# A four-layer graph network on one core: four pieces of work moved in the issue order

## The chip, the cores and the metric

The kernel runs on one core of a Trainium2 chip. The metric is the device time of one execution in microseconds (us), lower is better. All times below are from executions on the chip.

## The reference

The program takes `x` of 128 batches x 64 nodes x 256 features and an adjacency matrix `adj` (64 x 64), all float32. Four layers follow each other, each of the form

```python
h = jnp.maximum(_layernorm(x, axis=-1), 0.0)
x = x + layer(h)
```

Layer 0 is a graph convolution with batch normalization. Layer 1 multiplies with the eigenvectors of a normalized Laplacian, which the kernel computes itself. The change touches layers 2 and 3. Layer 2 is

```python
h = relu(einsum('ts,bsh->bth', adj, x @ Wg0 + bg0))
h = relu(einsum('ts,bsh->bth', adj, h @ Wg1 + bg1))
for p in range(1, 5):
    nw = 64 // p                      # windows of p consecutive nodes
    last = lstm(Wih[p-1], Whh[p-1], bias, h[:, :nw*p].reshape(-1, p, 256))   # the last state
    h = h.at[:, arange(nw)*p + (p-1)].set(last)
```

where the LSTM has gates i, f, g, o and zero initial state. So for p=1 each window is one node and needs the gates i, g and o alone, and for p=4 there are four cells in sequence. Layer 3 is an attention over 512 edges (`src`, `dst`) with 4 heads:

```python
Xq, Xv = H @ W_lin.T, H @ W_val.T                    # per head
e = (leaky_relu(Xq[src] + Xq[dst]) * a).sum(-1) + log(adj[src, dst] + 1e-8)
attn = exp(e - segment_max(e)[src]) / segment_sum(exp(..))[src]
Y = segment_sum(attn * Xv[dst], src)                 # then Y @ W_out.T
```

## The kernel before, in words

The 128 x 64 rows of `x` are kept in SBUF as 16 blocks of 512 rows (`NB` = 16 blocks, 8 batches each, tiles `X`), and are handled by block. In layer 2 they are also kept feature-major: `nodes(q)` gives a quarter of the batch (32 batches) as 128 features x 2 x 64 nodes x 32. A float32 product of two 256-wide operands is made from seven partial products instead of eight; they are made in the order 1, 6, 7, 5, 2, 4, 3 into four PSUM banks, with additions on VectorE (DVE) between. The sums of the operand that the seven products need are made ahead on DVE.

Instructions are recorded by a framework that orders them per engine by data dependencies and by the order in which they are written down. The wrapper `Ordered`/`Engines` stands around the engines, so that nearly all instructions of TensorE (PE), DVE and ScalarE (ACT) have one line in the profile, L800. `nc.mark()` returns the last instruction recorded on each of these three engines, and `nc.hold(marks)` makes what is recorded from then on go behind the marked one on its engine, without a semaphore.

The stages that matter:

- **Layer 2's two mixes** (`layer2`, to about 671 us). `block(i)` forms `g` of block i by the seven products with `W0` (`seven`; the last three products and their additions lie in the function `rest` that it returns, into the banks `ps` and `pe`), mixes block i-1's second half over the graph (`features(i-1)`, 16 small matmuls from `y` into `ps`), and multiplies `g` by `W1` into the bank `pt`, which gives `y`.
- **The LSTM** (`windows`, 671 to 1733 us). Its PSUM pools are `lsps` with seven banks, tile `ps`, and `lstps` with one bank, tile `pt`. For p=1, `single` handles the chunks in eight pairs; each pair has three groups of gates, and the multiplications of the cells lie on GpSimd (POOL). For p=2, 3 and 4, `lstm(p, t, ch, Ws)` is one cell of one chunk. It starts with the first sums `T` (tile `ls_tx`: one 128x512 and two 128x256 subtractions) of the nodes at step t, then makes the gates i and g, then o and f. The chunks are handled in pairs, t by t. For p=4 there are two pairs, so the second has eight cells (t = 0 to 3, two chunks).
- **The ways back.** `back(i)` takes block i of layer 2's result back to rows: ACT or DVE copies it to `ls_t`, TensorE transposes it in two times four 128x128 steps into `pt`, and DVE adds each four to `X`. Blocks 0 to 7 are done behind the cells of the second pair of p=4, from the list `ways`: one behind each cell with t < 2, two behind each with t = 2, which ends the list. Blocks 8 to 15 are done in layer 3's first steps.
- **Layer 3** (`layer3`, 1733 us to the end). Its PSUM pools are `l3ps` with seven banks and `l3cps` with one bank, tile `acc`. They take the place of `lsps` and `lstps`, bank by bank. `turned(0)` transposes the normalized block `h` twice into `acc` and copies it to `hT`, and `queries(0)` makes its first products with `w_qv` in `acc`, from which `XV` and `Q` are copied; all this is recorded with high priority. Then come 32 half-block steps g: `score` (edge scores from `ed_S` and `Q`), `reduce`, the values and the output. Each eight steps close a group q: `softmax(q)` is recorded in the last step of the group, and it works on 128x512 tiles `sm_e` and `sm_m`, with scans for the segment maximum and sum, then four reciprocals of 128x128 and one multiplication. Its result is read by `edgewise(q)`, recorded two steps later.

Of the kernel before, what the change touches and what calls it, by code (L numbers as in the profile page):

```python
# [843 lines left out]
class Plan:  # L844
# [56 lines left out]
    def rest(self):  # L901

        while any(self.queue.values()):
            for e in self.queue:
                self.fill(e, 1e9)
# [8 lines left out]
class Fast:  # L914
# [89 lines left out]
    def tridiagonal(self, S, made, plan):  # L1004
# [17 lines left out]

        d = go("T", lambda: keep("p", S, self.JR[:]), [made], 0.3, 0.5)
        d = go("V", lambda: o.copy(m[:], now["p"][:]), [d], 0.15, 0.28)
        d = go("T", lambda: keep("p", self.JR[:], m[:]), [d], 0.3, 0.5)
        rest = go("V", lambda: o.copy(A[:], now["p"][:]), [d], 0.15, 0.28)
# [419 lines left out]
NB = 16  # L1446
# [20 lines left out]
class Kernel:  # L1467
# [679 lines left out]
    def layer2(self, pool, psum, ps2, ps0):  # L2147

        nc, o = self.nc, self.o
# [89 lines left out]
        def block(i):  # L2239
            if i == 2:  # L2240
                with ExitStack() as ce:
                    epool = ce.enter_context(self.tc.tile_pool(name="l3e", bufs=1, side="right"))
                    nc.hold(nc.mark())
                    self.edges(self.w3, epool, ps0)
                    nc.hold()
            if i == SEVEN - 1:
                sums0()
            a = as_.pop(i)
            g = pool.tile([P, 2, BT], F32, name="g")
            rest = (seven if i >= SEVEN else eight)(i, a, g)  # L2250
            if i:
                features(i - 1)
            rest()
            mixed(i + 1)
            y = ys[i] = pool.tile([P, TPB, D], F32, name="y")
            for jj in range(0, TPB, 2):
                p = ps2.tile([P, 2, D], F32, name="pt")
                for j in range(2):
                    for kc in range(2):
                        self.mm(p[:, j, :], g[:, kc, (jj + j) * P:(jj + j + 1) * P], W1[:, kc, :],  # L2260
                                kc == 0, kc == 1)
                o.add(y[:, jj:jj + 2, :], p[:], b1[:, None, :].to_broadcast([P, 2, D]))
            normed(i + 2)
# [3 lines left out]
    def windows(self):  # L2267

        nc, o, io = self.nc, self.o, self.io
        cx, (w, wq, gp, tp, zp, psum, pst) = self.stage([("lsw", 1), ("lswq", 1), ("lsg", 2), ("lst", 2), ("lsz", 2),
                                                         ("lsps", 7), ("lstps", 1)], "tile")
        with cx:
            bias = w.tile([P, 4, 8], F32, name="ls_b")
            bh = w.tile([P, 4, 8], F32, name="ls_bh")
            with nc.allow_non_contiguous_dma("a few values"):
                nc.sync.dma_start(bias[:], io["L2_gnn_bih"].rearrange("q (k p) -> p q k", p=P))
                nc.sync.dma_start(bh[:], io["L2_gnn_bhh"].rearrange("q (k p) -> p q k", p=P))  # L2280
            o.add(bias[:], bias[:], bh[:])
            flat = [x.rearrange("p t d -> p (t d)") for x in self.X]
            self.late = []
            self.g_ = Ring([self.X2[i][:].rearrange("p x t d -> p x (t d)") for i in (4, 5, 6, 0)])
            self.t_ = Ring([flat[i] for i in (14, 2, 3)])
            self.c_, self.h_, self.th_ = Ring(flat[12:15]), Ring(flat[8:10]), Ring(flat[10:12])
            self.u_ = Ring([flat[15][:, 0:512], flat[15][:, 512:1024]])
            self.lp = gp, tp, zp, psum, bias

            def load(ap, n, x):  # L2290

                if x is None:
                    return ([wq.tile([P, 4 * D], F32, name=f"ls_w{n}{kc}")[:] for kc in range(2)]
                            + [wq.tile([P, 2 * D], F32, name=f"ls_s{n}{i}")[:] for i in range(3)])
                return [flat[x], flat[x + 1], flat[x + 2][:, 0:512], flat[x + 2][:, 512:1024], flat[x + 3][:, 0:512],
                        flat[x + 3][:, 512:1024]]

            def weights(p):

                out = []  # L2300
                for n, m in enumerate(("Wih", "Whh") if p > 1 else ("Wih",)):
                    t = load(None, n, None if p % 2 == 0 else 4 - 4 * n)
                    ap = io[f"L2_gnn_{m}_t"][p - 1]
                    for kc in range(2):
                        nc.sync.dma_start(t[kc], ap[kc * P:(kc + 1) * P, :])
                    A = [[t[kc].rearrange("p (x k m) -> p x k m", k=2, m=P)[:, :, k, :] for kc in range(2)]
                         for k in range(2)]
                    S1, S2, S4 = (y.rearrange("p (x m) -> p x m", m=P) for y in t[2:5])
                    o.add(S1, A[1][0], A[1][1])
                    o.sub(S2, S1, A[0][0])  # L2310
                    o.sub(S4, A[0][1], S2)
                    S3 = t[5].rearrange("p (x m) -> p x m", m=P) if len(t) > 5 else A[1][0]
                    o.sub(S3, A[0][0], A[1][0])
                    out.append({1: A[0][0], 2: A[0][1], 3: S4, 4: A[1][1], 5: S1, 6: S2, 7: S3})
                return out

            ready, ways = weights(1), []
            for p in range(1, 5):
                Ws = ready
                nw = N // p  # L2320
                parts = -(-nw // 16)
                chunks = []
                for q in range(NG):
                    w0 = 0
                    for k in range(parts):
                        w1 = w0 + (nw - w0) // (parts - k)
                        chunks.append((q, w0, w1))
                        w0 = w1
                for n in range(0, len(chunks), 2):
                    if n == 2 and p < 4:  # L2330
                        ready = weights(p + 1)
                    if n == 2 and p == 4:
                        self.fetch(0, 8)
                        ways = [0, 1, 2, 3, 4, 5, 6, 7]
                    two = [dict(q=q, w0=w0, w1=w1) for q, w0, w1 in chunks[n:n + 2]]
                    two[-1]["last"] = p == 4 and n + 2 >= len(chunks)
                    if p == 1:
                        self.single(two, Ws[0], n + 2 >= len(chunks))
                        continue
                    for t in range(p):  # L2340
                        for ch in two:
                            self.lstm(p, t, ch, Ws)
                            for i in ways[:1 if t < 2 else 2]:
                                self.back(i, pst, "pt")
                            ways = ways[1 if t < 2 else 2:]
            self.fetch(8, NB)

    def fetch(self, i0, i1):
# [15 lines left out]
    def lstm(self, p, t, ch, Ws):  # L2364


        o = self.o
# [6 lines left out]
        half = lambda kc: node(kc).rearrange("p w (h b) -> p h w b", h=2)  # L2374

        T = tp.tile([P, 4, 256], F32, name="ls_tx")[:, :, 0:W].rearrange("p n (w b) -> p n w b", b=16)
        o.sub(T[:, 0:2], H[:, :, at, 16:32], half(0))
        o.sub(T[:, 2], H[:, 1, at, 16:32], T[:, 0])
        o.sub(T[:, 3], H[:, 1, at, 0:16], T[:, 2])
        parts = [(Ws[0], {1: H[:, 0, at, 0:16], 2: H[:, 1, at, 0:16], 3: H[:, 1, at, 16:32],  # L2380
                          5: T[:, 0], 7: T[:, 1], 6: T[:, 2], 4: T[:, 3]})]
        if t:
# [222 lines left out]
    def layer3(self):  # L2605
        nc, o, io = self.nc, self.o, self.io
        cx, (w,) = self.stage([("l3x", 1)], "tile")
        with cx:
# [3 lines left out]
            with cy:  # L2612
# [10 lines left out]
                st, LAG = {}, 10  # L2623
# [4 lines left out]
                for g in range(8 * NG):  # L2628
# [22 lines left out]
                    if ahead:  # L2651
                        rest = self.queries(st, ahead, WQV, *pools)
                    elif g + 2 < 8 * NG:
                        self.turned(st, g // 2 + 1, *pools)
                    if g + 6 == 8 * NG:

                        p = pools[4].tile([P, BT], F32, name="ps")
# [2 lines left out]
                        self.act_copy(self.cont[:N, :], p[:N, :])  # L2660
                    if v >= 1 and g + 1 < 8 * NG:
                        self.output(st, v - 1, WO, *pools)
                    if g % 8 == 1 and 1 < g:
                        self.edgewise(st, g // 8 - 1, *pools)
                    if ahead:
# [198 lines left out]
    def softmax(self, st, q, pool, vp, sp, rp, psum, psc):  # L2864

        nc, o = self.nc, self.o
        e, m, m2 = self.shifted(st, q, pool, vp, sp, rp, psum, psc)
        scan = nc.vector.tensor_tensor_scan
        scan(m[:], self.cont[:], e[:], 0.0, op0=ALU.mult, op1=ALU.add)
        o.stt(m[:], self.contr[:], 0.0, m[:], ALU.is_equal, ALU.mult)  # L2870
        scan(m2[:, ::-1], self.contr[:, ::-1], m[:, ::-1], 0.0, op0=ALU.mult, op1=ALU.add)
        for c in range(4):
            o.recip(m2[:, c * P:(c + 1) * P], m2[:, c * P:(c + 1) * P])
        o.mul(e[:], e[:], m2[:])
        st["e", q] = e

    def summed(self, st, q, pool, vp, sp, rp, psum, psc):

# [148 lines left out]
```

## Time and profile before

| | |
|---|---|
| three runs | 2242.88, 2247.65, 2248.61 us |
| median | 2247.65 us |
| profiled execution | 2245.05 us |
| its span, first to last instruction | 2243.3 us |
| granted TensorE clock, mean | 0.997 |

| stage | us | TensorE busy |
|---|---|---|
| end of layer 2's mixes | 655 to 671 | 15.32 of 16.00 |
| p=1 | 671 to 822 | 147.43 of 151.00 |
| p=2 | 822 to 1092 | 270.00 of 270.00 |
| p=3 | 1092 to 1566 | 473.29 of 474.00 |
| p=4 | 1566 to 1733 | 165.84 of 167.00 |
| layer 3 | 1733 to 2243.3 | 504.68 of 510.30 |

The profile is one execution, recorded by the hardware. Times in it are microseconds from the span's start. In a timeline a line has the start, the duration, the engine, the source line, the operation, output<-input with the tiles' names, the shape, and the number of like instructions in a row that it stands for; in brackets stands the idle time of the engine before it and the engine and tile that ended that. In a list of waits a line has the engine and the tile that waited, what it waited for, the total, how often, and the longest. Matmuls are pipelined, so the durations of neighbours overlap.

### The profile page before, as it was taken

The numbers are of one execution on the slowest core, as the hardware profiler recorded it, in microseconds if no ns is written. First come the engines' busy times: TensorE is split into PE (matmuls) and PEld (weight loads), VectorE is DVE, ScalarE is ACT, GpSimd is POOL, SyncE is SP. The second block draws the span as 40 slices with busy tenths as digits, with TensorE's granted clock in tenths as the row PEclk, the third lists the DMA queues.
The fourth block names the chain that finished last, engine by engine and source line by source line (L and its number), as shares of the span: only waits on it lengthen the run. The fifth ranks groups of instructions, "written<-read, shape, count | busy, mean of one in ns | idle before, by whom it ended". The sixth has DMA issues, their size and how long they took to land.

```text
span 2243.3 us, 34321 instructions
## 1 busy us (share of the span) xinstructions
PE 2201.1 (98%) x12779; PEld 1644.5 (73%) x12779; DVE 1621.7 (72%) x4128; ACT 1154.4 (51%) x2522; POOL 127.5 (6%) x186
## 2 busy tenths in 40 slices
PE   7999998999999999999999999999999999999999
PEld 4554444667997888888999999888888645555654
DVE  8877576888757776676766776666767787877767
ACT  5667865665545663444444444334436654444431
POOL 1000000000225640000000000000000000000000
PEclk9999999999999999999999999999999999999999
DMA  6000220122000010000100002000001000000001
GB/s 182 1 1 15 72 57 23 64 76 41 1 29 1 1 38 1 1 1 1 39 1 1 1 1 75 2 1 1 13 1 62 20 1 15 20 15 20 15 25 48
DMA packets 61074, 54.92 MB, mean 24 GB/s; under 512 B 15203, under 2 KB 58724, under 8 KB 60900
## 3 DMA queue, kind: packets, MB, share of 16 engines
q1 hardware_dynamic: 60900, 52.66, 7.6%
q8 instruction: 102, 1.67, 0.3%
q14 instruction: 72, 0.59, 0.1%
HBM read 35.86 MB, written 16.78 MB: 23 GB/s over the span
## 4 chain that ended last, share of the span: by engine, by line
PE 77%; DVE 5%; ACT 1%; issue 1%; POOL 0%; DVEq 0%; ACTq 0%
PE ps L800 69%; PE pt L800 4%; PE acc L800 3%; PE pe L800 1%; DVE sm_m L800 1%; DVE X L800 1%; DVE aw L800 1%; DVE XV L800 0%; POOL big L2552 0%; ACT h L800 0%; ACT X L800 0%; ACT ls_g L800 0%; DVE ls_tx L800 0%; DVE lin_s L800 0%; ACT big L800 0%
## 5 line engine op out<-in xcount | busy, mean ns | idle before, releaser
L800 PE MATMUL ps<-X,X 128*128 128x160 f32 (+2 forms) x1302 | 296.7, 329 | 1.1 <-DVE X L800 0.9
L800 ACT ACTIVATE ls_g<-ls_g,ls_b 128x512 f32<-128x512 f32 (+5 forms) x408 | 207.8, 559 | 128.3 <-DVE ls_g L800 126.2
L800 PE MATMUL ps<-z,w 128*128 128x512 f32 x512 | 255.5, 621 | 0.0
L800 ACT ACTIVATE ls_g<-ps,ls_b 128x256 f32<-128x256 f32 (+2 forms) x204 | 80.5, 437 | 303.7 <-PE ps L800 302.5
L800 PEld LDWEIGHTS ps<-X,X 128*128 128x128 f32 x1302 | 225.2, 190 | 13.0 <-DVE X L800 2.7
L800 PE MATMUL ps<-X,ls_w 128*128 128x256 f32 x640 | 190.3, 379 | 0.0
L800 PE MATMUL ps<-big,X 128*128 128x256 f32 (+2 forms) x816 | 181.4, 333 | 2.6 <-ACT ls_z L800 2.5
L800 DVE TENSOR_TENSOR ls_g<-ls_z,ps 128x512 f32<-128x512 f32 (+3 forms) x226 | 125.2, 560 | 74.2 <-PE ps L800 72.4
L800 DVE TENSOR_TENSOR aw<-at,ed_OST 128x1024 f32<-128x1024 f32 x128 | 150.1, 1217 | 28.7 <-PE ps L800 28.5
L800 ACT ACTIVATE r<-ps 128x512 f32<-128x512 f32 x256 | 129.3, 625 | 74.4 <-PE ps L800 74.3
L800 PEld LDWEIGHTS ps<-big,X 128*128 128x128 f32 x816 | 139.7, 190 | 11.6 <-ACT ls_z L800 3.5
L800 PE MATMUL ps<-ls_tx,X 128*128 128x160 f32 (+1 forms) x704 | 146.2, 307 | 0.6 <-ACT ls_g L800 0.6
L800 DVE TENSOR_TENSOR X<-ls_z,ps 128x512 f32<-128x512 f32 (+4 forms) x185 | 112.4, 608 | 42.6 <-PE ps L800 37.5
L800 PE MATMUL ps<-X,ls_s 128*128 128x256 f32 x480 | 142.7, 379 | 0.0
L800 PEld LDWEIGHTS ps<-z,w 128*128 128x128 f32 x512 | 86.9, 190 | 66.6 <-issue 59.0
L800 PE MATMUL ps<-ls_tx,ls_s 128*128 128x256 f32 x464 | 134.9, 379 | 0.9 <-DVE ls_tx L800 0.9
L800 PE MATMUL ps<-ls_tx,ls_w 128*128 128x256 f32 x464 | 133.2, 380 | 0.0
L800 PEld LDWEIGHTS ps<-X,ls_w 128*128 128x128 f32 x640 | 121.2, 190 | 16.3
L800 PE MATMUL ps<-big,ls_w 128*128 128x256 f32 x464 | 131.4, 379 | 0.0
L800 DVE TENSOR_TENSOR X<-ls_g 128x1024 f32<-128x1024 f32 (+2 forms) x92 | 97.7, 1062 | 38.1 <-ACT ls_g L800 37.9
L800 PE MATMUL ps<-ed_S,Q 64*128 64x512 f32 x512 | 121.0, 604 | 0.9 <-DVE X L800 0.9
L800 PE MATMUL ps<-aw,ed_ODT 128*32 128x512 f32 x1024 | 121.7, 593 | 0.1
(583 smaller groups left out, 4203.0 us busy)
## 6 DMA issues: line engine op xcount, KB each, us to landing
X<-in_x_dram SPq DMA_DIRECT2D x32, 512.0 KB
xs<-X SPq DMA_DIRECT2D x16, 512.0 KB
X<-xs SPq DMA_DIRECT2D x16, 512.0 KB
out_dram<-X SPq DMA_DIRECT2D x31, 256.0 KB
X<-in_L_gnn_Wih_t_dram SPq DMA_DIRECT2D x4, 512.0 KB
ls_w<-in_L_gnn_Wih_t_dram SPq DMA_DIRECT2D x4, 512.0 KB
ls_w<-in_L_gnn_Whh_t_dram SPq DMA_DIRECT2D x4, 512.0 KB
w<-in_L_gnn_W_t_dram SPq DMA_DIRECT2D x2, 512.0 KB
```

Of the source, the lines that this page charges most:

```text
L800: i = method(*a, **kw)
```

## The change

Four places are changed; the instructions stay the same in number and kind.

1. In the last block of layer 2's mixes, `rest()` is recorded ahead of `features(i - 1)` instead of behind it.
2. The first sums of the first pair of p=2 are held on DVE until what was recorded ahead of p=1's last pair is issued.
3. The four reciprocals and the multiplication of `softmax` become a function `divided`, recorded in the next step of layer 3 and held on DVE behind what was recorded there before.
4. One `back(i)` is recorded behind each of the eight cells of the last pair of p=4.

```diff
             rest = (seven if i >= SEVEN else eight)(i, a, g)
+            if i == NB - 1:
+                rest()
             if i:
                 features(i - 1)
-            rest()
+            if i < NB - 1:
+                rest()
             mixed(i + 1)
...
                     if p == 1:
+                        if n + 2 >= len(chunks):
+                            after = nc.mark()[1]
                         self.single(two, Ws[0], n + 2 >= len(chunks))
                         continue
+                    if p == 2 and n == 0:
+                        for ch in two:
+                            ch["after"] = after
                     for t in range(p):
                         for ch in two:
                             self.lstm(p, t, ch, Ws)
-                            for i in ways[:1 if t < 2 else 2]:
+                            for i in ways[:1]:
                                 self.back(i, pst, "pt")
-                            ways = ways[1 if t < 2 else 2:]
+                            ways = ways[1:]
...
         T = tp.tile([P, 4, 256], F32, name="ls_tx")[:, :, 0:W].rearrange("p n (w b) -> p n w b", b=16)
+        self.nc.hold((None, ch.get("after"), None))
         o.sub(T[:, 0:2], H[:, :, at, 16:32], half(0))
         o.sub(T[:, 2], H[:, 1, at, 16:32], T[:, 0])
         o.sub(T[:, 3], H[:, 1, at, 0:16], T[:, 2])
+        self.nc.hold()
...
+                    if g % 8 == 0 and g:
+                        self.divided(st, g // 8 - 1)
                     if g % 8 == 1 and 1 < g:
                         self.edgewise(st, g // 8 - 1, *pools)
...
         scan(m2[:, ::-1], self.contr[:, ::-1], m[:, ::-1], 0.0, op0=ALU.mult, op1=ALU.add)
+        st["e", q], st["sums", -1] = e, m2
+
+    def divided(self, st, q):
+
+        nc, o, e, m2 = self.nc, self.o, st["e", q], st["sums", -1]
+        nc.hold((None, nc.mark()[1], None))
         for c in range(4):
             o.recip(m2[:, c * P:(c + 1) * P], m2[:, c * P:(c + 1) * P])
         o.mul(e[:], e[:], m2[:])
-        st["e", q] = e
+        nc.hold()
```

## The prediction

> **What bounds the kernel now.** First the page: the engine table and, in its fourth part, the chain that ended last.
>
> ```profile
> PE 2201.1 (98%) x12779; PEld 1644.5 (73%) x12779; DVE 1621.7 (72%) x4128; ACT 1154.4 (51%) x2522; POOL 127.5 (6%) x186
> PE 77%; DVE 5%; ACT 1%; issue 1%; POOL 0%; DVEq 0%; ACTq 0%
> ```
>
> TensorE is the bound. An edit gains only where a matmul waits, and loses only where it makes one wait. So the second view is TensorE's waits from 640 us on, the part with all four edits (total, times, longest).
>
> ```profile
> PE ps L800 <- ACT ls_z L800: 2.5, 2, 1.3
> PE ps L800 <- DVE X L800: 1.9, 5, 0.5
> PE ps L800 <- DVE hS L800: 0.7, 1, 0.7
> PE pt L800 <- DVE g L800: 0.7, 1, 0.7
> ```
>
> Every edit has its stall here, and all are small. I size them in the timelines by start-to-start gaps: a 128x256 matmul issues every 0.215 us there (pairs 0.43 apart), so four take 0.86, and four transposes 0.43.
>
> **Part 1, last mix of layer 2.** The third product pair starts at 665.14; the next matmul, the output's, waits for the last `g` until 666.42: 1.28 for 0.43 of work, 0.85 idle. The change puts the 16 matmuls of `features(14)`, 16 x 0.108 to 0.12 = 1.7 to 1.9 us, into that gap. `features` itself reads a `y` that is ready. No DMA moves. Product 3 may now wait 0.06 for its bank. Gain 0.8 (0 to 0.9). If that cover were gone, the 0.85 would stay.
>
> **Part 2, first sums of p=2.** DVE's timeline and TensorE's row, in the second single pair:
>
> ```profile
> 697.29 1.19 DVE L800 TENSOR_TENSOR ls_tx<-big 128x512 f32<-128x512 f32 x1 [1.87 <-POOL big L2552]
> 699.57 1.33 ACT L800 ACTIVATE X<-X,ls_b 128x512 f32<-128x512 f32 x2 [4.19 <-DVE X L800]
> 701.44 1.13 PE L800 MATMUL ps<-big,X 128*128 128x256 f32 x4 [1.31 <-ACT ls_z L800]
> ```
>
> The sums wait 1.87 for GpSimd's multiplication, and behind them in DVE's queue stand the gate additions, behind those ScalarE's gates, and behind those the copy that TensorE wants. Start-to-start excess: 1.48 and 0.55 here, 1.34 and 0.54 in the next pair (the second chunk's sums, which wait 2.33). The sum is 3.91, and 0.1 more lies in small waits. Pairs without these sums show none of it, so I take -4.0 (-3.9 to -4.1). The sums are paid again ahead of the last single pair: DVE idles 1.11 before its addition at 805.57 and 1.04 before 808.95, and gets 2 x (1.19 + 0.42 + 0.42) = 4.1 us of sums. An overhang of 4.1 - 2.15 = 1.95 stays; in the first groups TensorE runs one bank ahead, so I take +0.3 (0 to +1.5, most of the overhang). Their operand was written by GpSimd 100 us before, so no wait comes with them. On GpSimd and SyncE nothing is moved.
>
> **Part 3, softmax.** The division is four reciprocals and a multiplication:
>
> ```profile
> 1828.34 3.38 DVE L800 RECIPROCAL sm_m<-sm_m 128x128 f32<-128x128 f32 x4
> 1833.53 1.97 PE L800 MATMUL ps<-w_t,hS 128*128 128x256 f32 x8 [0.70 <-DVE hS L800]
> ```
>
> The sums `hS` that TensorE waits for stand behind these 4.1 us. The change puts them ahead. Excess there 0.87, in the second and third group 0.62 each, and 0.15 in a small wait: 2.26. What is late next is ScalarE's `XV` in the first, about 0.3, so -1.9 (-2.3 to 0). The division's reader, the transposes of `sm_e` in the next odd step, comes after the scores and queries, 4 us and more of matmuls, which hide it; without that cover the 4.1 would come back three times.
>
> **Part 4, one way back per cell.** Two gains: the second way back behind the t=2 cells stalls the transposes by 0.29 and 0.30 (rows at 1659.45 and 1685.71: 0.73 start-to-start for 0.43). Gain 0.6 (0.5 to 0.6). And one cost. The eighth way back now follows the very last cell. Layer 3's first transposes go into the one-bank pool `l3cps`, which takes the bank of `lstps`, where the ways back put theirs. Before, layer 3's start was spread over the last cells:
>
> ```profile
> 1696.57 0.60 PE L800 MATMUL acc<-ident,h 128*128 128x128 f32 x4
> 1700.89 1.03 PE L800 MATMUL acc<-w_qv,hT 128*128 128x256 f32 x4
> ...
> 1697.27 0.59 ACT L800 ACTIVATE hT<-acc 128x512 f32<-128x512 f32 x1
> 1699.37 0.60 ACT L800 ACTIVATE XV<-acc 128x512 f32<-128x512 f32 x1
> 1701.96 0.60 ACT L800 ACTIVATE Q<-acc 128x512 f32<-128x512 f32 x1 [1.99 <-PE acc L800]
> ```
>
> In the changed kernel's instruction order these 12 matmuls come behind all of the LSTM's, with a wait in front of each four, and the first scores behind them wait for `Q`. I add the chain up from t=0, the start of the last product's two rows (1732.46 before). Latencies are from rows: transposes to reader 0.43 + 0.27 = 0.70, `w_qv` to reader 1.07 (1700.89 to 1701.96), a crossing back 0.06 more. The last gate addition (after three row statistics, 0.36 each) ends at 1.9; the first half of the product `big` (0.67) at 2.6; the addition of the way back's first four transposes (0.6) at 3.2; its second four transposes at 3.9; the second half of `big`, a row statistic and the second addition at 4.7; `acc` transposes 5.5; DVE's `hT` copy 6.2; `acc` transposes 6.9; ScalarE's `hT` copy 7.5; `w_qv` 8.6; `XV` copy 9.2; `w_qv` 10.3; `Q` copy 10.9; score at 11.0. TensorE has of its own in that stretch 0.86 + 0.54 + 0.86 + 1.72 = 3.98. So it waits 7.0 (5.5 if statistics and second half overlap with the chain, 8.5 if every crossing costs 0.15 more). The row statistics that come with the late ways back put about 0.3 more on the last gates. Layer 3 doesn't give it back:
>
> ```profile
> 1733.00:1850.00 117.00, 116.01 (x655) 64.35 (x654) 92.37 (x204) 75.72 (x141) 0.00 (x0) 1.00 0.07 21
> ```
>
> TensorE is busy 116.01 of these 117 us (first column after the width). The DMAs of X 8 to 15 keep their place on SyncE, behind the last cell.
>
> **The clock behind that wait** has no row of its own. The nearest rows, from the windows (columns: TensorE, weight loads, DVE, ScalarE, GpSimd busy, then the granted clock):
>
> ```profile
> 113.50:115.00 1.50, 0.55 (x6) 0.30 (x5) 1.02 (x6) 1.14 (x5) 0.00 (x0) 1.00 0.00 0
> 116.50:118.00 1.50, 1.50 (x6) 0.66 (x5) 0.73 (x4) 0.27 (x2) 0.00 (x0) 0.50 0.00 0
> ...
> 364.50:369.80 5.30, 0.27 (x2) 0.19 (x3) 0.77 (x8) 0.40 (x2) 0.00 (x0) 0.85 0.06 9
> 369.80:375.00 5.20, 5.17 (x23) 4.93 (x24) 2.03 (x11) 3.10 (x5) 0.00 (x0) 0.50 0.41 129
> ...
> 398.50:400.25 1.75, 0.45 (x4) 0.46 (x4) 1.75 (x6) 1.11 (x3) 0.00 (x0) 1.00 0.54 188
> ```
>
> A 0.95 us gap was followed by some 3.4 us at 0.50, worth 1.7; the 5 us gap by 5.2 us, and later 3.4 more (382 to 385.4), worth 4.3; 396.75 to 400.25, busy 1.27 of 3.5, by none, and the 1.3 us stalls of part 2 by none. The wait here is in pieces, busy 4 of 11. I take one spell, +1.7, nearest to the first row (0 to +5.1, three spells).
>
> The Trainium skill ("TensorE: Matmul & The Clock Gate", Part 1, What's actually happening) says that the rate halves only after a whole idle window of about 3.4 us. By it no piece of this wait is long enough and the term would be 0, the sum +0.3. The row at 116.50 speaks against it: 0.50 after a gap of 0.95.
>
> **Sum:** -0.8 - 4.0 + 0.3 - 1.9 - 0.6 + 7.0 + 0.3 + 1.7 = +2.0. The profiled execution took 2245.05 (span 2243.3, 1.75 around it), so it would become 2247.0. It lies 2.6 below the median of the runs, 2247.65; for the median I add the same 2.0: **2249.6**. What one measurement of this kernel tells from no change is about 0.3%, 6.7 us; the runs of before spread over 5.7.
>
> **Rivals.** *Slower:* the seam is long and runs at half clock. At 8.5 with three spells it costs 8.5 + 0.3 + 5.1 = 13.9 instead of 9.0, net +6.9, 2254.5. For: the rows at 369.8; the chain crosses between engines more than ten times. Against: TensorE is never idle for 5 us at once. It decides from a seam of 13.7 on. *Faster:* the seam costs nothing, because the last way back ends before the last gates are through and layer 3's transposes flow in. Then the three seam terms (9.0) fall, net -7.0, 2240.6. It decides below 0.3 of seam. For: four gains that are each seen as stalls. Against: the waits in the order written for the engines, and `big`, which needs the last gate. *The change does not do what it says:* its holds could be undone by the scheduler, giving 2247.7; the changed kernel's order shows all four moves, so this has 0.02.
>
> **Chances and range.** Likeliest case, seam 7 to 11 with its clock: 0.64, own range 2245.5 to 2253.5. Slower rival 0.22, faster rival 0.12, no effect 0.02. The range goes from 2241, where half of the faster rival lies, to 2256, past the slower rival's price by 1.5; about 2 in 10 stay out. Faster by over 0.3%: 0.12; within: 0.64 + 0.02 = 0.66; slower: 0.22.
>
> **What would show it.** Right: no DVE wait for GpSimd's `big` by `ls_tx`, no TensorE wait for `g` or `hS`, `ls_tx` rows at about 800 with under 0.5 of waits behind them, no pause at the p=4, t=2 transposes, and TensorE idle about 7 us between the last LSTM rows and the first `ed_S,Q` scores, in waits for DVE `X` and `hT` and ScalarE `hT`, `XV`, `Q`. Wrong: a seam under 3 or over 10 us, more than one stretch at 0.50 behind it, or waits over 1 us where the sums or the division now stand.

## The result and the profile after

The changed kernel takes 2251.51 us (median of 13 runs, 2246.56 to 2253.73) against 2245.33 of the kernel before (13 runs beside them, 2242.49 to 2248.61): ratio 1.0024, 95% interval 1.0016 to 1.0031, that is 3.6 to 7.0 us slower. The ratio lies inside the 0.3%, and the median inside the range. The profiled executions differ by 4.1 us (span 2247.4 against 2243.3).

The sum hides large terms of both signs. TensorE's waits from 640 us on, after (total, times, longest):

```profile
PE pt L800 <- DVE X L800: 1.8, 1, 1.8
PE ps L800 <- ACT big L800: 1.5, 1, 1.5
PE acc L800 <- DVE X L800: 0.9, 1, 0.9
PE acc L800 <- DVE hT L800: 0.8, 1, 0.8
PE acc L800 <- ACT hT L800: 0.7, 1, 0.7
PE acc L800 <- ACT XV L800: 0.7, 1, 0.7
PE ps L800 <- ACT Q L800: 0.7, 1, 0.7
```

The waits for `ls_z`, `g` and `hS` are gone, as forecast. The five lines with `acc` and `Q` and the first one with `pt` are the seam between the LSTM and layer 3. The line with ScalarE's `big` was not forecast.

Where the time goes is best read by setting the start of the same matmul in both traces against each other:

| matmul | before | after | later by | step |
|---|---|---|---|---|
| last block of layer 2, first product | 660.33 | 660.51 | 0.18 | ahead of the change |
| first of the LSTM | 671.48 | 672.57 | 1.09 | part 1: **+0.9** |
| behind the second sums (pair 3) | 723.50 | 720.32 | -3.18 | part 2: **-4.3** |
| end of p=2 | 1092.81 | 1089.40 | -3.41 | the sums' new place: **-0.2** |
| last product's rows | 1732.46 | 1725.56 | -6.90 | 3.12 of it is work that the order moved behind: **-0.4** |
| first score of layer 3 | 1733.42 | 1739.03 | 5.61 | the seam: 5.61 + 3.78 = **+9.4** |
| scores behind it | 1736.10 | 1744.13 | 8.03 | half clock behind it: **+2.4** |
| behind the third division | 2071.97 | 2075.87 | 3.90 | part 3: **-4.1** |

(The 3.12 are sixteen `acc` matmuls and five transposes of the last way back: 8 x 0.108 + 8 x 0.215 + 5 x 0.108.) The steps and the 0.18 ahead of them come to 3.9, and the last 0.2 lie at the end.

At part 2's place the matmul that stood at 701.44 before, with a wait of 1.31 for `ls_z`, stands at 701.11 here, without one:

```profile
698.52 2.75 PE L800 MATMUL ps<-X,X 128*128 128x256 f32 x12
701.11 1.03 PE L800 MATMUL ps<-big,X 128*128 128x256 f32 x4
```

The seam in the timeline of the changed kernel, TensorE's rows (the last row ends with the window asked for, at 1742; the group goes on):

```profile
1725.56 0.60 PE L800 MATMUL ps<-big,ls_s 128*128 128x256 f32 x2
1728.49 0.66 PE L800 MATMUL pt<-ident,ls_t 128*128 128x128 f32 x4 [1.79 <-DVE X L800]
1730.02 0.91 PE L800 MATMUL acc<-ident,h 128*128 128x128 f32 x4 [0.87 <-DVE X L800]
1731.71 1.12 PE L800 MATMUL acc<-ident,h 128*128 128x128 f32 x4 [0.78 <-DVE hT L800]
1733.51 2.07 PE L800 MATMUL acc<-w_qv,hT 128*128 128x256 f32 x4 [0.69 <-ACT hT L800]
1736.27 2.07 PE L800 MATMUL acc<-w_qv,hT 128*128 128x256 f32 x4 [0.69 <-ACT XV L800]
1739.03 3.78 PE L800 MATMUL ps<-ed_S,Q 64*128 64x512 f32 x8 [0.69 <-ACT Q L800]
```

The chain is the one that the prediction wrote down, link by link. But from 1730 on the rows are twice as long: four `w_qv` took 1.03 before and take 2.07 here. The windows (first column after the width TensorE busy, then weight loads, DVE, ScalarE, GpSimd, the granted clock) show why:

```profile
1726.85:1730.26 3.41, 0.90 (x6) 0.67 (x7) 3.41 (x8) 1.58 (x2) 0.00 (x0) 1.00 0.79 245
1730.26:1743.90 13.64, 10.80 (x28) 5.53 (x28) 2.36 (x6) 3.96 (x8) 0.00 (x0) 0.50 0.34 111
```

The stretch at 0.50 lasts 13.65 us, where one spell of 3.4 had been taken. The seam itself, from the last product's rows to the first score, takes 13.47 us (1725.56 to 1739.03).

### The profile page after: what moved, and what is told of

It reads as the page before. It is cut to its first block, busy times and chain, and to the rows that moved or that the text cites. A ratio compares the mean times of both kernels' runs of the same rounds, so it can differ in the third digit from the quotient of the medians.

```text
span 2247.4 us, 34325 instructions
## 1 busy us (share of the span) xinstructions
PE 2203.9 (98%) x12779; PEld 1648.8 (73%) x12779; DVE 1622.1 (72%) x4128; ACT 1154.6 (51%) x2522; POOL 128.9 (6%) x186
## 4 chain that ended last, share of the span: by engine, by line
PE 80%; DVE 2%; ACT 1%; issue 0%; DMA 0%; ACTq 0%; DVEq 0%
PE ps L800 71%; PE pt L800 4%; PE acc L800 3%; PE pe L800 1%; DVE X L800 1%; ACT h L800 0%; DVE aw L800 0%; ACT big L800 0%; ACT r L800 0%; DMA ls_w<-in_L_gnn_Wih_t_dram 0%; DVE n_st L800 0%; DVE ls_s L800 0%; ACT ls_g L800 0%; DVE XV L800 0%; DVE big L800 0%
```

## The experiments

**Part 4 undone.**

```diff
-                            for i in ways[:1]:
+                            for i in ways[:1 if t < 2 else 2]:
                                 self.back(i, pst, "pt")
-                            ways = ways[1:]
+                            ways = ways[1 if t < 2 else 2:]
```

> The changed kernel with part 4 undone: two ways back behind the cells with t=2, as before; parts 1 to 3 as changed. Theory (the seam from the LSTM to layer 3 and the half clock behind it cost about 11.9 us in the changed profile, and part 4 gains 0.6 at t=2): this is about 11 us faster than the changed kernel and 7 us faster than before (2238), the first scores start 0.96 us after the last product's rows as before, and no half-rate spell lies at the start of layer 3. Rival (the loss lies in the other three parts, for instance at the seam's own DMAs): no more than 4 us faster than the changed kernel.

Measured: 2235.55 us, ratio to before 0.9964 (0.9951 to 0.9978), 8 us faster than before. TensorE's rows at the seam are those of before, 0.95 from the last product's rows to the first score, and no half clock:

```profile
1726.83 0.60 PE L800 MATMUL ps<-big,ls_s 128*128 128x256 f32 x2
1727.78 2.42 PE L800 MATMUL ps<-ed_S,Q 64*128 64x512 f32 x10
```

So parts 1 to 3 together gain, and part 4 more than takes it back. The rival falls.

**Part 4 alone.** On the kernel before, the loop of the change's last diff lines alone.

```diff
-                            for i in ways[:1 if t < 2 else 2]:
+                            for i in ways[:1]:
                                 self.back(i, pst, "pt")
-                            ways = ways[1 if t < 2 else 2:]
+                            ways = ways[1:]
```

> Part 4 alone on the kernel before. Theory: the seam with its clock stands alone, 11 to 12 us slower than before less 0.6, so about 2256.5, ratio 1.005. Rival (the seam only costs what the prediction summed, 9 us less 0.6): 2253.7. The profile decides by the distance from the last product's rows to the first score (13.5 against 11) and by the length of the stretch at 0.50 (13 us against 3.4).

Measured: 2257.18 us, ratio 1.0056 (1.0042 to 1.0069). The seam takes 13.54 us, and 13.65 us lie at half clock. Both as in the changed kernel, so nothing in the other parts is needed for it. The rival's 8.4 us are a ratio of 1.0037, just below the interval; the two rows of the profile that were named beforehand decide against it clearly.

**The last way back in another bank.**

```diff
-                                self.back(i, pst, "pt")
+                                self.back(i, *((psum, "ps") if i == 7 else (pst, "pt")))
```

> The changed kernel, still one way back behind each cell, but the eighth puts its transposes into the LSTM's seven-bank pool instead of the one bank that layer 3 starts in. Theory (the one shared bank is what holds layer 3's start behind the last cell): layer 3's first transposes and products lie among the last cell's again, the seam falls to under 2 us, no half-rate spell, 11 to 12 us faster than the changed kernel, about 8 faster than before. Rival (it is the place of the last way back, its copies and additions on DVE, that delays layer 3): the seam stays over 5 us and the time within 5 us of the changed kernel.

Measured: 2238.19 us, ratio 0.9968 (0.9957 to 0.9980). Layer 3's first transposes and products lie among the last cell's matmuls again (two of their rows first), the last way back stands among the last gates, and the scores follow:

```profile
1716.53 0.60 PE L800 MATMUL acc<-ident,h 128*128 128x128 f32 x4
1720.10 1.03 PE L800 MATMUL acc<-w_qv,hT 128*128 128x256 f32 x4
...
1727.43 0.93 PE L800 MATMUL ps<-ident,ls_t 128*128 128x128 f32 x7
1729.12 0.27 PE L800 MATMUL ps<-ident,ls_t 128*128 128x128 f32 x1
1729.23 0.62 PE L800 MATMUL ps<-big,ls_s 128*128 128x256 f32 x2
1729.68 0.59 PE L800 MATMUL ps<-X,ls_s 128*128 128x256 f32 x2
1730.40 1.99 PE L800 MATMUL ps<-ed_S,Q 64*128 64x512 f32 x8
```

The seam is 1.17 (1729.23 to 1730.40), and no half clock lies there. One line moves the result from slower to faster, without touching what is computed or where a way back is recorded. The single bank that `lstps` hands to `l3cps` is the cause, not the copies and additions of the way back: those are still there.

**The seam filled with matmuls.** Groups of matmuls that nobody reads stand in TensorE's waits, held in place by the marks; without them the kernel is the changed one.

```diff
+    def fill(self, p, a, b, n):
+        self.hold((self.mark()[0], None, None))
+        for _ in range(n):
+            self.tensor.matmul(p, a, b, start=True, stop=True, skip_group_check=True)
+        self.hold((self.mark()[0], None, None))
...
+            self.filled(jj == 2)               # 4, ahead of the last four transposes of the last way back
...
+            self.filled()                      # 2, ahead of each acc step and of the first score
```

> The changed kernel with 14 additional matmuls (128x512, read by nobody) placed in TensorE's waits of the seam: four ahead of the last four transposes of the way back, two ahead of each of the next five steps. Nothing else is changed. Theory (of the 11.9 us at the seam about 7 are the chain of waits and about 4.9 the half clock, in the seam and behind it): no stretch at 0.50, first score 11.0 to 11.5 us after the last product's rows instead of 13.5, and 4 to 5 us faster than the changed kernel. Rival (the clock falls for another reason than the waits): the stretch stays, and the time is the same or up to 3 us slower.

Measured: 2250.05 us, ratio 1.0022 (1.0012 to 1.0031), no gain. The clock did stay at 1.00, but the first score came 16.13 after the last product's rows. My filling was too large: such a matmul stands as two rows of 0.43 in the trace, so that it takes 0.86, and two of them overran each gap. The run shows that the waits draw the clock down, and nothing on its price. So again with half the columns:

```diff
-            self.nc.fill(p, self.ident[:], self.logA[:], n)
+            self.nc.fill(p[:, 0:256], self.ident[:], self.logA[:, 0:256], n)
```

> As the run with 14 additional matmuls in the seam, each with half the columns (128x256). In that run one of them took 0.86, not the 0.43 that I had planned, and so the filling itself was on the path: the clock stayed at 1.00, but the first score came 16.1 us after the last product's rows. Theory (about 7 us of waits, the rest clock): still no stretch at 0.50, the first score after 10.8 to 12 us, and 3 to 5 us faster than the changed kernel. Rival (the loss of clock costs nothing that the chain does not cost anyway): first score at 13 us or later, and no difference from the changed kernel.

Measured: 2246.40 us, ratio to before 0.9998 (0.9989 to 1.0007). The windows, and some of TensorE's rows:

```profile
1723.32:1734.30 10.98, 10.92 (x56) 8.25 (x54) 7.07 (x17) 4.65 (x7) 0.00 (x0) 1.00 0.76 253
```

```profile
1727.78 0.66 PE L800 MATMUL acc<-ident,h 128*128 128x128 f32 x4
1728.27 1.03 PE L800 MATMUL ps<-ed_log,ident 128*128 128x256 f32 x4
1730.57 1.11 PE L800 MATMUL acc<-w_qv,hT 128*128 128x256 f32 x4
1734.30 1.13 PE L800 MATMUL ps<-ed_S,Q 64*128 64x512 f32 x4
```

At full clock the seam takes 10.98. In the changed kernel it takes 13.47, and 2.42 more are lost behind it. So the half clock costs 13.47 - 10.98 + 2.42 = 4.9 us, and the waits proper 10.98 - 3.98 = 7.0. The added matmuls leave TensorE hardly any idle time (busy 10.92 of 10.98), so they may set the pace by a little: the copy of `Q` ends at 1734.14 and the first score starts at 1734.30. The 7.0 is good to some tenths, and rather high. More work on TensorE makes this kernel faster, by 0.0026 in the ratios, 5.8 us (that estimate carries some 3 us from the two intervals).

**Part 1 alone.** On the kernel before, `rest()` ahead of `features(i - 1)` in the last block:

```diff
+            if i == NB - 1:
+                rest()
             if i:
                 features(i - 1)
-            rest()
+            if i < NB - 1:
+                rest()
```

> Part 1 alone on the kernel before. Theory (the wait for g goes, and the last relu's bank, now bank 0, holds the LSTM's first product): the output's matmuls follow without a pause (-0.6 to -0.85), the first LSTM matmul waits about 1.5 for ScalarE's big, net 0.9 to 1.2 later at the LSTM's second group of matmuls than in the kernel before. Rival (the new wait comes from another part, the sums or a DMA): net -0.6 to -0.85. The time itself cannot tell these apart; the profile's rows do.

Measured once: 2243.72 us (2246.19 before, 15 runs, which spread over 6.7). TensorE's rows:

```profile
665.73 1.03 PE L800 MATMUL pt<-w,g 128*128 128x256 f32 x4
666.60 2.10 PE L800 MATMUL ps<-BDA,y 128*128 128x128 f32 x16
670.22 1.13 PE L800 MATMUL ps<-big,X 128*128 128x256 f32 x4 [1.52 <-ACT big L800]
```

This execution had two half-clock spells fewer in layers 0 and 1 and runs 2.17 us ahead at the last block's first product (658.16 against 660.33), ahead of any part of the change. Against that, the first LSTM matmul stands at -1.26 + 2.17 = 0.91 later than before, with the same wait of 1.5 as in the changed kernel. The reason was read from the built program, since no trace shows bank numbers. In its bank assignment the last mix takes banks 3 and 2 before, and 1 and 0 after: a bank goes to who asks next in the order in which the banks come free, and the earlier `rest()` frees its two banks ahead of those of `features(14)`. The LSTM's first product takes bank 0 in both. It now waits until ScalarE has read the last mix out of it (1.88 for two). That a bank and not the data holds it, the mended version below shows: there the last mix's first half takes a bank of another pool, and the wait is gone.

**Part 3 alone.** On the kernel before, `softmax` split and `divided` called as in the change:

```diff
+                    if g % 8 == 0 and g:
+                        self.divided(st, g // 8 - 1)
```

> Part 3 alone on the kernel before. Theory (three groups, each with a stall that brackets show and one hidden within a merged row of scores): TensorE's rows from 1815 on end 3.5 to 4.2 us earlier against the kernel before, 0.7 to 1.0 of it in the first group and 1.2 to 1.7 in each of the others; the second group's sixteen scores go in one row of 3.7 us. Rival (the prediction's 1.9, the rest comes from what the seam shifted): 1.9 to 2.3 earlier.

Measured once: 2241.53 us. TensorE's rows end 3.6 us earlier than before: 0.8 in the first group, some 1.5 in the second, 1.3 in the third. The rest of the changed kernel is not needed for this. The second group, in this run's timeline:

```profile
1942.98 3.70 PE L800 MATMUL ps<-ed_S,Q 64*128 64x512 f32 x16
```

and the same scores in the timeline of the kernel before:

```profile
1943.66 3.81 PE L800 MATMUL ps<-ed_S,Q 64*128 64x512 f32 x12
1947.94 1.13 PE L800 MATMUL ps<-ed_S,Q 64*128 64x512 f32 x4 [0.46 <-DVE X L800]
```

Before, twelve scores took as long as sixteen do now. A row that stands for several instructions shows a wait only if it lies ahead of the first of them: 1.0 us of waiting lay inside `x12`.

**A mended version.** Parts 2 and 3 as changed; the last mix's first half in the output's bank pool; the list of ways ends one cell earlier.

```diff
-    def mix(self, psum, h, bd, out, paired=False):
+    def mix(self, psum, h, bd, out, paired=False, first=None):
...
-            p = psum.tile([P, BT], F32, name="ps")
+            p = psum.tile([P, BT], F32, name="ps") if dc or not first else first[0].tile([P, BT], F32, name=first[1])
...
+                first=(ps2, "pt") if i == NB - 1 else None)
...
-                            for i in ways[:1]:
+                            k = 2 if ways and t == 2 and ch is two[1] else 1
+                            for i in ways[:k]:
                                 self.back(i, pst, "pt")
-                            ways = ways[1:]
+                            ways = ways[k:]
```

> A version that keeps what gains: parts 2 and 3 as changed; part 1 with the first half of the last mix put into the output's bank pool, so that the LSTM's first three products take banks that nobody reads any more; and part 4 with two ways back behind the second cell with t=2, so that the list ends one cell earlier. Theory (bank 0's wait and the seam are the only two losses): the first LSTM matmul does not wait, layer 3's start lies among the last cell's matmuls, no half-rate spell there; -0.6 - 4.2 - 0.3 - 3.8 = -8.9 against before, about 2235, ratio 0.996. Rival (bank waits turn up elsewhere, as in part 1): between the changed kernel with part 4 undone (-8.4) and before.

Measured: 2236.61 us, ratio 0.9953 (0.9940 to 0.9967), 7 to 13 us faster than before and the fastest ratio of all, though its interval overlaps that of the changed kernel without part 4. TensorE's waits from 640 us on are down to four lines:

```profile
PE ps L800 <- DVE ls_tx L800: 0.9, 1, 0.9
PE ps L800 <- ACT ls_g L800: 0.6, 1, 0.6
PE ps L800 <- DVE X L800: 0.3, 2, 0.2
PE acc L800 <- ACT XV L800: 0.3, 1, 0.3
```

The first LSTM product starts at 673.34 without a wait, behind the last mix at 672.89.

**All profiles from the same matmul on.** The executions stand up to 2.6 us apart from the kernel before when the change begins. So here is the time from the last block's first product (660.33 before) to the end of the span, one execution each, against the kernel before:

| run | us |
|---|---|
| the changed kernel | +3.9 |
| part 4 undone (parts 1 to 3) | -7.1 |
| part 4 alone | +11.0 |
| last way back in another bank | -6.9 |
| seam filled, 128x512 | +4.2 |
| seam filled, 128x256 | -0.9 |
| part 1 alone | +0.8 |
| part 3 alone | -3.7 |
| mended version | -8.6 |

Parts 1 to 3 and part 4 add up to the changed kernel. The filling of the seam gains 4.8, which agrees with the 4.9 worked out for the half clock. Part 2 has no run of its own; -7.1 less the parts 1 and 3 leaves -4.2 for it.

## Why the prediction came out as it did

The median came 1.9 us above the forecast of 2249.6. Some of that nearness is luck. The forecast added its +2.0 to a median of three runs, 2247.65, and the thirteen runs of before came to 2245.33; the difference is 5.4 by the ratio, 6.2 by the medians and 3.9 in the profiles, where 2.0 was forecast. And three terms failed, part 1 by +1.7, part 3 by -2.2 and the clock by +3.2, so that they partly cancelled. One of the prediction's own signs of being wrong came true: a seam over 10 us. It took 13.47, just short of the 13.7 from which the slower rival decides.

- **Part 1, the sign was wrong.** "Gain 0.8 (0 to 0.9)" became a loss of 0.9. The stall for `g` went as forecast (the last mix starts 0.78 earlier, counted from the block's first product), and the cover held. (The row at 665.14 is the output's first pair; the third product starts at 664.71. The 0.85 of idle time stands.) What failed is "Product 3 may now wait 0.06 for its bank" as the only wait: I asked who waits for the moved matmuls' data, and not who gets the banks that they free. The bound was open on the wrong side too.
- **Part 2** was right: -4.0 forecast, -4.3 in the trace of the changed kernel. The charge of +0.3 at the new place was not paid. The sums stand between the last pair's additions from 801.20 on, and TensorE has no wait from 799 to 823.
- **Part 3, mis-sized:** -1.9 (-2.3 to 0) became -4.1 in the changed kernel and -3.6 alone. The step that failed is the reading of the scores' rows by their brackets, which hid some 1.0 in the second group and 0.7 in the third. The first group gave 0.8; whether 0.3 for `XV` was lost there no row shows.
- **Part 4 at t=2:** -0.6 forecast together with 0.3 for the late row statistics, -0.4 measured for both.
- **The seam:** 11.0 for the chain, of which 7.0 are waits; 10.98 and 7.0 in the filled run. (Layer 3's matmuls behind the LSTM are sixteen, not the 12 of the text; the sum counts sixteen.) The third experiment shows its cause, the shared bank. This is why the faster rival didn't come.
- **The clock, mis-sized:** +1.7 was taken and 4.9 came, near the end of 5.1 that the slower rival used. So the slower rival was right on the size of the clock term (from three spells; four units came, in which TensorE was busy 10.80 of 13.64 us) and wrong on the length of the chain (8.5). I chose the row at 116.50 as "nearest"; but there TensorE was busy 2.25 of the 3.40 us before the spell, and in the seam 0.90 of 3.41. The nearer row by that measure was the one at 364.5. Both rows were also read too short, because their windows cut them: the gap of "0.95" is 1.15 in the timeline (114.05 to 115.20), and the "5.2 us" at half clock were 6.83. What failed is that one spell was taken without asking what brings the clock back; in the seam it came back only after four units of 3.41 us (the last section has the rows).
- The rule weighed beside it (the Trainium skill, "TensorE: Matmul & The Clock Gate", What's actually happening: half rate after a whole idle window) would have given 0. No window of 3.41 us in the seam was idle throughout, and the clock halved. The same page's section "A second HAM failure mode: psum-queue depth-cycling" tells of frequent short idles that draw the clock down, and that agrees with the row of 0.90 of 3.41 and with the filled runs.

## What to carry over

When an edit moves the last user of a PSUM bank, list the next owner of each bank that it frees or keeps, across the border of the stages: here one shared bank cost 11.8 us and another a wait of 1.5, and in each case a change of bank took it away. Size a stall by the start-to-start time over the whole group of matmuls, since a merged row shows only the wait ahead of its first. And price a pause of TensorE with the clock behind it: the six waits of the seam, with little work between them, cost 7.0 us at full clock and another 4.9 by the loss of it.

## What the hardware showed

The half clock comes in whole units: the stretches at 0.50 within the traces lasted 3.41, 6.83, 10.24 or 13.65 us. In the changed kernel the four units of the seam were

```profile
1730.26:1733.67 3.41, 1.94 (x9) 1.14 (x7) 1.69 (x5) 0.64 (x2) 0.00 (x0) 0.50 1.00 325
1733.67:1737.09 3.42, 2.73 (x6) 1.74 (x7) 0.67 (x2) 0.60 (x1) 0.00 (x0) 0.50 0.33 116
1737.09:1740.50 3.41, 2.72 (x7) 1.29 (x8) 0.00 (x0) 0.60 (x1) 0.00 (x0) 0.50 0.01 2
1740.50:1743.90 3.40, 3.40 (x10) 1.36 (x8) 0.00 (x0) 2.12 (x4) 0.00 (x0) 0.50 0.00 0
```

With TensorE busy 1.94, 2.73 and 2.72 the clock stayed at 0.50; behind the unit that was busy throughout it came back. So it is in all ten traces, cut into such units from 20 us on: behind none of the 17 half-clock units busy up to 0.80 did the clock come back, and behind 23 of the 24 busy 0.95 or more it did.

A window of 3.41 with TensorE busy 0.90 was followed by half clock, in the changed kernel and, at a busy share of 0.25, with part 4 alone; a window of 1.84 in 3.40 (719.8 to 723.2, before) was not. Counted over the ten traces, all 13 full-clock units with a busy share up to 0.37 were followed by half clock, and none of the 39 between 0.45 and 0.65. But the share does not decide alone: of the 25 units between 0.66 and 0.69 ten were followed by it, and of the units above none. Two windows of layer 0 around the same pause, from the kernel before:

```profile
112.30:115.70 3.40, 2.25 (x22) 1.94 (x22) 2.42 (x16) 3.01 (x10) 0.00 (x0) 0.99 0.00 0
115.70:119.10 3.40, 3.40 (x8) 1.31 (x8) 1.76 (x9) 2.03 (x9) 0.00 (x0) 0.50 0.02 5
```

and from those of the run with part 1 alone:

```profile
113.60:117.00 3.40, 2.25 (x16) 1.23 (x15) 2.68 (x15) 2.86 (x10) 0.00 (x0) 1.00 0.02 5
117.00:120.40 3.40, 3.40 (x16) 1.59 (x15) 2.30 (x11) 2.77 (x9) 0.00 (x0) 1.00 0.01 2
```

The busy share is the same, 2.25 of 3.40, and only one of them loses the clock; the two cut the program at different places, so they do not hold quite the same matmuls. At the last block of layer 2, before any edit can act on it, the profiled executions stand up to 2.6 us ahead of the kernel before or behind it, and they differ in spells of this kind in layers 0 and 1. That is of the size of the scatter of the runs (13 of before between 2242.49 and 2248.61); that it is its whole cause was not tested. What decides between 0.66 and 0.69 stays open.
